# Reordering the opening of a fused attention and feed-forward kernel, and moving two centrings from ScalarE to GpSimd

## The chip, the cores and the metric

The kernel runs on one core of one Trainium2 chip. A core has five engines that each work through their own list of instructions in order and wait for each other through semaphores: TensorE (PE, matrix products; PEld is its weight load), VectorE (DVE), ScalarE (ACT), GpSimd (POOL) and SyncE (SP, which only issues transfers here). The metric is the device time of one launch in microseconds (us); lower is better.

## What is computed

With `x` of 2048 rows by 256, a context of 1601 rows by 192 and 16 heads of 64:

```python
x = x + xattn(layernorm(x), context, mask)   # 16 heads; one learned null key and value in front: 1602 keys
x = x + ffn(layernorm(x))                    # three layers with weights +1/-1: 256 -> 1024 -> 1024 -> 256

# xattn: q = (layer_norm(x) * g_norm) @ Wq ; k, v = split(context @ Wkv)
#        out = softmax(q k^T * 64**-0.5, masked) @ v @ Wout, then layer_norm(out) * g_out
```

Everything is float32 (`fp32r` marks operands rounded for a faster matrix product).

## The kernel before

**Tiling.** The 16 heads are taken as 8 pairs (p), the 2048 rows as 4 blocks (b) of 512: 32 units (p, b), in the order of the list `units`. The 1602 keys are 13 tiles of 128 (KC = 13; the last holds 66). For every unit the kernel needs, ahead of time, an upper bound of each row's scores, so that the exponential does not overflow. These maxima are computed by rounded products in chunks of 512 keys (`max_chunk`, TensorE line 400, then a reduction on VectorE, line 403). Chunk n belongs to query tile n // 3 and key chunk n % 3; `REST` (12) is the last 66 keys of all four tiles.

**One unit of the main loop** (from line 679 on) runs over the 13 key tiles. In step k TensorE writes the scores of a key tile (`scores`, line 442) into one of two buffers `sT`, ScalarE takes the exponential (`exps`, line 468) into one of 13 buffers `e`, TensorE computes one maximum chunk of the *next* unit, and GpSimd adds `e` into the accumulator `acc` for the softmax denominator (lines 720 and 722 inside the loop for tiles 1 to 7, line 728 after it for tile 0 and tiles 8 to 12). The score buffers alternate, so the scores of step k + 2 cannot start before the exponential of step k is done. Tile 0 of the exponentials holds the last, partly filled key tile and is first multiplied on ScalarE by the factor `spent` (line 726). After the loop follow the weighted values (`weighted`, line 475, 52 products), the division by the denominator of the unit before, its output projection, and the projections for coming units.

**What orders the work.** All engines' orders are written out by hand inside `manual_schedule()`; nothing is planned. Two one-element copies to `seen` on ScalarE are there for their waits. The second (line 711) reads one element of the *previous* unit's `acc`, and as ScalarE works in order, everything behind it waits until the last addition into that `acc` is done. It stands before step k = 2 in units 3 to 27 and before step k = 8 in the others (line 710).

**The denominator** of the previous unit is handled in one of two ways (line 746). `quarters` puts it across partitions by `denominators` (line 499), a reciprocal of 256 columns (line 511) and eight copies on ScalarE (line 517). Otherwise `divided` (line 524) makes it with wider products, three key tiles into the weighted values, and one reciprocal of 512 columns (line 526). Before, unit 1 uses `divided`.

**The opening** (lines 629 to 678) prepares unit (0, 0): the keys in three pieces (`first_keys`), the values in two halves (`values_begun`, `values_ended`), the maxima of block 0 in between, and the centring of row block 1 (`second_summed` on ScalarE, `second_normed` on GpSimd). Blocks 2 and 3 are centred in units 0 and 1: VectorE sums them (`input_root`), ScalarE takes the root (a table load, line 535), and `centred_beside` (lines 145 and 146) subtracts and scales with eight ScalarE instructions. `input_turned` (line 556) then transposes the block on TensorE at the end of the same unit. `masked_counted` (lines 428 to 432) counts masked keys by a small product, a VectorE reduction and three GpSimd instructions, and gives `spent`; before, it is the last step of the opening. The maxima use two PSUM buffers (`flex`); keys, values, transposes and scores of the opening share two others (`spare`).

Of the kernel before, what the change touches and what calls it, by code (L numbers as in the profile page):

```python
# [12 lines left out]
AF = mybir.ActivationFunctionType  # L13
# [25 lines left out]
def xattn_ffn(ctx, tc, x, ctxT, mask, g_norm, null_kv, wq, wkv, wout, g_out, k0, k1, k2, s0, s1, s2, out):  # L39
# [108 lines left out]
    with ExitStack() as att:  # L148
# [46 lines left out]
        def project_q(p, b, get=flex, part=None):  # L195

            if part is not None:
                if part == 0:
                    halves["q"] = get(f"psq_{p}_{b}")
                ps = halves["q"]  # L200
                nc.tensor.matmul(
                    ps[:, 0, :], weights[p][0][:, part, :], xnT[:, b, part, :], start=part == 0, stop=part == 1
                )
                if part == 0:
                    return
            qT = wp.tile([128, 512], F32, tag="qT", name=f"qT_{p}_{b}")
            qr = wp.tile([128, 512], F32R, tag="qr", name=f"qr_{p}_{b}", bufs=1)
            if part is None:
                ps = get(f"psq_{p}_{b}")
            for c in range(2) if part is None else ():  # L210
                nc.tensor.matmul(ps[:, 0, :], weights[p][0][:, c, :], xnT[:, b, c, :], start=c == 0, stop=c == 1)  # L211
            nc.scalar.mul(qr, ps[:, 0, :], DH**-0.5)  # L212
            nc.scalar.mul(qT, ps[:, 0, :], DH**-0.5)
            queries[p, b] = (qT, qr)
# [19 lines left out]
        def first_keys(n, get, part=None):  # L234

            kT, _, kr = pairs[0]
            chunks = (CHUNKS[1], CHUNKS[2]) if n == 1 else (CHUNKS[n],)
            if part != 1:
                halves["k"] = get(f"psk_0_{n}")
            ps = halves["k"]  # L240
            for i, (start, w) in enumerate(chunks):
                if part is None or part == i:
                    nc.tensor.matmul(
                        ps[:, i, :w], weights[0][1][:, 0, :], ctx_a[:, ds(start, w)], start=True, stop=False
                    )
            if part == 0:
# [50 lines left out]

        halves = {}

        def values_begun(p, m, tiles, get=flex):  # L300

            if (p, m) not in halves:
                halves[p, m] = get(f"psv_{p}_{m}").rearrange("p i (t d) -> p (i t) d", d=128)
            for t in tiles:
                nc.tensor.matmul(  # L305
                    halves[p, m][:, t - 8 * m, :],
                    ctx_a[:, ts(t, 128)],
                    weights[p][1][:, 1, :],
                    start=t % 4 == 0,
                    stop=False,  # L310
                    skip_group_check=True,
                )

        def values_ended(p, m):

            v, pv = pairs[p][1], halves[p, m]
            tiles = range(8 * m, min(8 * m + 8, KC))
            for t in sorted(tiles, key=lambda t: (t % 4, t)):
                rows = ts((t - 8 * m) // 4, 64)
                nc.tensor.matmul(  # L320
                    pv[:, t - 8 * m, :],
                    ctx_b[rows, ts(t, 128)],
                    weights[p][2][rows, 1, :],
                    start=False,
                    stop=True,
                    skip_group_check=True,
                )
            w = len(tiles)
            nc.scalar.copy(v[:, ds(8 * m, w), :], pv[:, :w, :])
            if p > 0 and m == 0:  # L330
                nc.gpsimd.tensor_copy(v[0:1, 0, :], nullv)

# [5 lines left out]
        def second_summed():  # L338

            sums = sp.tile([128, 2, 4], F32, tag="sums", name="sums_1", bufs=1)  # L340
            r = sp.tile([128, 4], F32, tag="rstd", name="rstd_x1")
            aside = wp.tile([128, D], F32, tag="aside", name="aside", bufs=1)
            for j in range(4):
                nc.scalar.activation(aside, x_sb[:, 4 + j, :], AF.Identity, accum_out=sums[:, 0, j : j + 1])
            nc.gpsimd.tensor_scalar(sums[:, 0, :], sums[:, 0, :], -1.0 / D, None, ALU.mult)
            for j in range(4):
                nc.scalar.activation(
                    aside, x_sb[:, 4 + j, :], AF.Square, bias=sums[:, 0, j : j + 1], accum_out=sums[:, 1, j : j + 1]
                )
            nc.scalar.activation(r, sums[:, 1, :], AF.Sqrt, bias=eps2_sb, scale=(1.0 + EPS) / D)  # L350
            return sums, r
# [289 lines left out]
        first_queries(1)  # L641
        nc.gpsimd.tensor_copy(kept[:, : KC - 1], mcol_u8[:, : KC - 1])
        nc.gpsimd.tensor_copy(kept[:KLAST, KC - 1 : KC], mcol_u8[:KLAST, KC - 1 : KC])
        mv, r = second_summed()
        max_chunk(0, 0, 6)
        first_keys(1, spare, 0)
        max_chunk(0, 0, 9)
        first_keys(1, spare, 1)
        values_begun(0, 0, range(0, 8), spare)
        max_chunk(0, 0, 1)  # L650
        nc.vector.reciprocal(r, r)
        second_normed(mv, r)
        nc.scalar.activation(warm, eps_sb, AF.Exp)
        max_chunk(0, 0, 4)
        values_ended(0, 0)
        max_chunk(0, 0, 7)
        first_keys(3, spare)
        max_chunk(0, 0, 10)
        values_begun(0, 1, range(8, KC), spare)
        max_chunk(0, 0, 2)  # L660
        values_ended(0, 1)
        max_chunk(0, 0, 5)
        keys_stepped(0)
        values_masked(0, 0)
        values_masked(0, 1)
        input_turned(1, spare)
        max_chunk(0, 0, 8)
        max_chunk(0, 0, 11)
        project_q(0, 1, spare)
        max_chunk(0, 0, REST)  # L670
        odd = spare("sT_0_0_1")
        sT = [spare("sT_0_0_0"), odd]
        scores(0, 0, 1, sT[1])
        max_combined(0, 0)
        max_turned(0, 0)
        scores(0, 0, 0, sT[0])
        masked_counted(flex)
        begin.__exit__(None, None, None)
        last = None
        with tc.manual_schedule():  # L680
            for u, (p, b) in enumerate(units):
# [25 lines left out]

                    nc.scalar.copy(seen[:, 0:1], before[:1, 0, 0:1])
                for k in range(KC):
                    if k == (2 if 2 < u < len(units) - 4 else 8) and last is not None:  # L710
                        nc.scalar.copy(seen[:, 1:2], last[3][:1, 0, 0:1])
                    if k == 0 and u > 0:

                        odd = spare(f"sT_{p}_{b}_1")
                        sT = [spare(f"sT_{p}_{b}_0"), odd]
                    es.append(exps(p, b, k, sT))
                    if nxt is not None:
                        max_chunk(*nxt, order[k])
                    if k == 2:
                        nc.gpsimd.tensor_tensor(acc, es[1], es[2], ALU.add)  # L720
                    elif 2 < k < 8:
                        nc.gpsimd.tensor_tensor(acc, acc, es[k], ALU.add)  # L722
                if nxt is not None:
                    max_combined(*nxt)

                nc.scalar.mul(es[0][64:], es[0][64:], spent[64:, 0:1])
                for k in (0, *range(8, KC)):
                    nc.gpsimd.tensor_tensor(acc, acc, es[k], ALU.add)  # L728
                if nxt is None:
                    norm_begin(0, x_sb, "r")  # L730
                    norm_root(0)
                    norm_end(0, y_sb, x_sb, beside=True)
                if u == len(units) - 2:
# [2 lines left out]
                    norm_end(0, y_sb, y_sb, beside=True)  # L736

                    nc.scalar.activation(warm, eps_sb, AF.Exp)
                if u < 2:
                    input_normed(u + 2, *input_root(u + 2), beside=True)  # L740
                    nc.scalar.activation(warm, eps_sb, AF.Exp)
                if u == 0:
                    nc.sync.dma_start(out=ctx_b[64:, 1:512], in_=ctxT[128:CD, 0:511])


                quarters = last is not None and u not in (1, len(units) - 2, len(units) - 1)
                if quarters:
                    den = flex(f"den_{p}_{b}")[:, 0, :256]
                    denominators(last[3], den)
# [204 lines left out]
```

## Time and profile before

| | us |
|---|---|
| median of 3 runs (1269.84 to 1270.65) | 1270.56 |
| the profiled execution, its own time | 1270.18 |
| its span, first to last instruction | 1268.4 |
| TensorE busy | 1257.9 (99%) |
| GpSimd busy | 1008.5 (80%) |
| VectorE busy | 761.7 (60%) |
| ScalarE busy | 717.9 (57%) |

How to read it: times in a timeline count from the span's start. A row of a timeline joins equal instructions that follow each other; its first number is when the first one starts, the second how long the whole row lasts, and behind "x" stands how many there are. A plain float32 product of TensorE shows as two passes, so `x104` at line 475 is 52 products; a rounded one (fp32r) shows as one. In brackets stands the idle time of the engine before the row, and who ended it. A row of waits gives engine and line, then who was waited for, then the total, the number and the longest.

### The profile page before, as it was taken

How to read it: one execution, taken by the hardware profiler on the slowest of the kernel's cores; microseconds unless marked ns; L12 is line 12 of the kernel's file. 1: busy time of each engine (PE TensorE's matmuls, PEld its weight loads, DVE VectorE, ACT ScalarE, POOL GpSimd, SP SyncE). 2: the span in 40 equal slices, each digit the busy share in tenths (PEclk: the TensorE clock that was granted, in tenths of full speed). 3: DMA queues.
4: the chain of work that ended last, by engine and by line, in shares of the span. 5: the costliest groups of instructions: out<-in, count | busy, mean ns of one | idle time of the engine just before them, and what ended most of it. 6: DMA issues, size and time to landing. Idle time of an engine off the chain costs nothing.

```text
span 1268.4 us, 19642 instructions
## 1 busy us (share of the span) xinstructions
PE 1257.9 (99%) x8332; PEld 644.0 (51%) x8332; DVE 761.7 (60%) x812; ACT 717.9 (57%) x982; POOL 1008.5 (80%) x515
## 2 busy tenths in 40 slices
PE   8999999999999999999999999999999999999998
PEld 5344444444444444444444444444444443788887
DVE  6687766656665566556655666656666793635431
ACT  4776666666666656665666566666666676322120
POOL 5898999899889988998899988998898999701100
PEclk9999999999999999999999999999999999999999
DMA  6000000000000000000000000000000010000000
GB/s 171 1 1 5 1 1 13 5 1 1 13 5 1 1 14 5 1 1 13 5 1 2 13 5 1 1 1 6 1 17 1 1 42 1 1 17 1 17 17 17
DMA packets 16984, 13.46 MB, mean 11 GB/s; under 512 B 3152, under 2 KB 16336, under 8 KB 16896
## 3 DMA queue, kind: packets, MB, share of 16 engines
q1 hardware_dynamic: 15904, 11.21, 3.2%
q8 instruction: 65, 1.06, 0.4%
q10 hardware_dynamic: 656, 0.79, 0.2%
q0 software_dynamic: 336, 0.21, 0.1%
q14 instruction: 23, 0.19, 0.0%
HBM read 10.11 MB, written 2.10 MB: 10 GB/s over the span
## 4 chain that ended last, share of the span: by engine, by line
PE 95%; POOL 2%; ACT 1%; DMA 1%; issue 0%; DVE 0%; SPq 0%; DVEq 0%; POOLq 0%; ACTq 0%
PE sT L442 28%; PE av L475 27%; PE ps L836 12%; PE max L400 7%; PE psq L211 4%; PE po L488 4%; PE ps L867 2%; PE psv L305 2%; PE psk L270 1%; PE den L499 1%; PE sT L466 1%; PE psv L320 1%; POOL acc L728 1%; PE psk L275 1%; PE max L384 1%; PE mt L413 1%
## 5 line engine op out<-in xcount | busy, mean ns | idle before, releaser
L403 DVE TENSOR_REDUCE mx<-max 128x2 f32<-128x1024 f32 x384 | 444.4, 1218 | 86.0 <-PE max L400 82.3
L728 POOL TENSOR_TENSOR acc<-acc,e 128x1024 f32<-128x1024 f32 x192 | 473.1, 2464 | 15.1
L468 ACT ACTIVATE e<-sT 128x1024 f32<-128x1024 f32 x416 | 425.8, 1024 | 87.7 <-PE sT L466 44.3
L442 PE MATMUL sT<-qT,kT 64*128 64x512 f32 x1664 | 444.8, 608 | 1.6 <-ACT e L468 1.3
L722 POOL TENSOR_TENSOR acc<-acc,e 128x1024 f32<-128x1024 f32 x160 | 379.3, 2371 | 12.6
L475 PE MATMUL av<-e,v 128*32 128x512 f32 x3328 | 363.6, 592 | 0.1
L400 PE MATMUL max<-kr,qr 64*128 64x512 f32 x768 | 280.6, 718 | 1.2 <-ACT qr L227 1.0
L475 PEld LDWEIGHTS av<-e,v 128*32 128x32 f32 x3328 | 107.4, 110 | 237.9 <-issue 230.1
L442 PEld LDWEIGHTS sT<-qT,kT 64*128 64x128 f32 x1664 | 134.0, 185 | 132.6 <-ACT e L468 121.0
L720 POOL TENSOR_TENSOR acc<-e,e 128x1024 f32<-128x1024 f32 x32 | 75.6, 2363 | 59.6 <-ACT e L468 59.6
L400 PEld LDWEIGHTS max<-kr,qr 64*128 64x128 f32 x768 | 76.7, 187 | 88.6 <-DVE mx L403 65.2
L517 ACT COPY aoT<-r 32x256 f32<-32x256 f32 x224 | 90.2, 403 | 33.4 <-DVE r L511 31.1
L782 ACT COPY avs<-av 128x512 f32<-128x512 f32 x32 | 18.8, 587 | 145.8 <-PE av L475 145.8
L415 DVE TENSOR_TENSOR mT<-mt,pick 128x512 fp32r<-128x512 f32 x32 | 22.1, 690 | 113.4 <-PE mt L413 112.9
L518 DVE TENSOR_TENSOR aoT<-avs,aoT 128x512 f32<-128x512 f32 x28 | 33.3, 1189 | 94.4 <-ACT aoT L517 94.4
L836 PE MATMUL ps<-h0hi,w 128*128 128x512 f32 x256 | 79.6, 392 | 0.0
L836 PE MATMUL ps<-h0lo,w 128*128 128x512 f32 x256 | 78.9, 389 | 0.0
L124 POOL TENSOR_TENSOR y_sb<-y_sb,gout_sb 128x256 f32<-128x256 f32 x12 | 9.3, 777 | 85.6 <-DVE y_sb L91 85.6
L824 ACT ACTIVATE h1hi<-ps 128x1024 fp32r<-128x1024 f32 x16 | 16.4, 1027 | 99.2 <-PE ps L836 99.2
L212 ACT ACTIVATE qr<-psq 128x512 fp32r<-128x512 f32 x31 | 18.5, 598 | 93.5 <-PE psq L211 91.4
L488 PE MATMUL po<-wo,aoT 128*128 128x256 f32 x256 | 60.5, 379 | 0.0
L825 DVE SCALAR_TENSOR_TENSOR h1lo<-ps,h1hi 128x1024 fp32r<-128x1024 f32 x16 | 19.6, 1224 | 67.0 <-ACT h1hi L824 67.0
(171 smaller groups left out, 1207.8 us busy)
## 6 DMA issues: line engine op xcount, KB each, us to landing
out_x<-o SPq DMA_DIRECT2D x7, 256.0 KB, 2.1
x_sb<-in_x SPq DMA_DIRECT2D x3, 512.0 KB, 5.2
wa<-in_wkv SPq DMA_DIRECT2D x8, 128.0 KB, 2.9
wb<-in_wkv SPq DMA_DIRECT2D x16, 64.0 KB, 2.5
wq<-in_wq SPq DMA_DIRECT2D x8, 128.0 KB, 2.2
wo<-in_wout SPq DMA_DIRECT2D x8, 128.0 KB, 2.1
xnT<-in_k SPq DMA_DIRECT2D x1, 1024.0 KB, 5.7
ctx_a<-in_ctxT SPq DMA_DIRECT2D x2, 256.0 KB, 6.2
```

What stands on the lines that cost most here:

```text
L211: nc.tensor.matmul(ps[:, 0, :], weights[p][0][:, c, :], xnT[:, b, c, :], start=c == 0, stop=c == 1)
L400: nc.tensor.matmul(ps[:, j, :w], qr[rows, ts(t, 128)], kr[rows, ds(start, w)], start=True, stop=True)
L403: nc.vector.tensor_reduce(maxima[p, b][:, t, :, c], ps[:, :, :w], AX.X, ALU.max)
L442: nc.tensor.matmul(ps[:n, j, :], kT[rows, ds(128 * KEY_TILES[k], n)], qT[rows, :], start=k < 2, stop=k >= 2, skip_group_check=k >= 2,)
L468: nc.scalar.activation(e, ps, AF.Exp)
L475: nc.tensor.matmul(av[ts(i, 32), 0, :], v[:n, KEY_TILES[k], ts(i, 32)], e[:n, i // 2, :], start=k == 1, stop=k == 0, tile_position=(0, 32 ...
L488: nc.tensor.matmul(pv[:, t, :], aoT[:, ts(t, 128)], weights[p][3], start=True, stop=True)
L517: nc.scalar.copy(aoT[ds(64 * j + 32 * rows, 32), ts(h, 256)], r[ds(64 * j + 32 * h, 32), :])
L720: nc.gpsimd.tensor_tensor(acc, es[1], es[2], ALU.add)
L722: nc.gpsimd.tensor_tensor(acc, acc, es[k], ALU.add)
L728: nc.gpsimd.tensor_tensor(acc, acc, es[k], ALU.add)
L836: nc.tensor.matmul(ps[:, f, :], w(c)[:, ts(2 * g + f, 128)], parts[part][:, c, :], start=i == 0, stop=i == len(steps) - 1,)
```

## The change

It has five parts.

1. *Opening, order on TensorE.* `first_keys(1)` is called in three parts, around maximum chunks 6 and 9: the first 512 keys come ahead of chunk 6. Chunks 1 and 4 follow each other, and the first half of the values is begun with six tiles ahead of them and two behind. Chunk 2 moves ahead of the second half of the values. The query projection of block 1 is cut in two around chunk `REST`.
2. *Opening, other engines.* The reciprocal for block 1 and `second_normed` move behind chunk 7. The table load for the exponential moves from ahead of the first value copy to behind the last one. The five last value tiles are placed in PSUM as three and two (`places`), so that three row pairs finish them, and are copied in two pieces.
3. *`masked_counted`* leaves the opening and comes after the loop over key tiles of unit 0.
4. *Blocks 2 and 3* (the third and fourth) are centred by four GpSimd instructions that stand behind the addition of tile 0; ScalarE keeps the root and the two table loads.
5. *`seen`* is copied at k = 2 in units 1, 2 and 28 too, and unit 1 uses `quarters`.

The transfers and their order on SyncE and GpSimd stay as they are.

```diff
         first_queries(1)
...
+        first_keys(1, spare, 0)
         mv, r = second_summed()
         max_chunk(0, 0, 6)
-        first_keys(1, spare, 0)
+        first_keys(1, spare, 1)
         max_chunk(0, 0, 9)
-        first_keys(1, spare, 1)
-        values_begun(0, 0, range(0, 8), spare)
+        first_keys(1, spare, 2)
+        values_begun(0, 0, range(0, 6), spare)
         max_chunk(0, 0, 1)
+        max_chunk(0, 0, 4)
+        values_begun(0, 0, range(6, 8), spare)
+        values_ended(0, 0)
+        max_chunk(0, 0, 7)
         nc.vector.reciprocal(r, r)
         second_normed(mv, r)
-        nc.scalar.activation(warm, eps_sb, AF.Exp)
-        max_chunk(0, 0, 4)
-        values_ended(0, 0)
-        max_chunk(0, 0, 7)
         first_keys(3, spare)
         max_chunk(0, 0, 10)
+        max_chunk(0, 0, 2)
         values_begun(0, 1, range(8, KC), spare)
-        max_chunk(0, 0, 2)
+        max_chunk(0, 0, 5)
         values_ended(0, 1)
-        max_chunk(0, 0, 5)
+        nc.scalar.activation(warm, eps_sb, AF.Exp)
...
-        project_q(0, 1, spare)
+        project_q(0, 1, spare, 0)
         max_chunk(0, 0, REST)
+        project_q(0, 1, spare, 1)
...
-        masked_counted(flex)
...
-                    if k == (2 if 2 < u < len(units) - 4 else 8) and last is not None:
+                    if k == (2 if u < len(units) - 3 else 8) and last is not None:
                         nc.scalar.copy(seen[:, 1:2], last[3][:1, 0, 0:1])
...
+                if u == 0:
+                    masked_counted(flex)
                 if nxt is not None:
                     max_combined(*nxt)
 
                 nc.scalar.mul(es[0][64:], es[0][64:], spent[64:, 0:1])
+                if u < 2:
+                    mv, r = input_root(u + 2)
+                    nc.vector.reciprocal(r, r)
+                    nc.scalar.activation(warm, eps_sb, AF.Exp)
                 for k in (0, *range(8, KC)):
                     nc.gpsimd.tensor_tensor(acc, acc, es[k], ALU.add)
+                    if k == 0 and u < 2:
+                        for j in range(4):
+                            t = 4 * (u + 2) + j
+                            nc.gpsimd.tensor_scalar(
+                                y_sb[:, t, :], x_sb[:, t, :], mv[:, j, 0:1], r[:, j : j + 1], ALU.subtract, ALU.mult
+                            )
...
-                if u < 2:
-                    input_normed(u + 2, *input_root(u + 2), beside=True)
-                    nc.scalar.activation(warm, eps_sb, AF.Exp)
...
-                quarters = last is not None and u not in (1, len(units) - 2, len(units) - 1)
+                quarters = last is not None and u not in (len(units) - 2, len(units) - 1)
```

More of the change, by code (lines that the diff above doesn't have):

```diff
@@ L237, in first_keys @@
             chunks = (CHUNKS[1], CHUNKS[2]) if n == 1 else (CHUNKS[n],)
-            if part != 1:
+            if not part:
                 halves["k"] = get(f"psk_0_{n}")
@@ L245, in first_keys @@
                     )
-            if part == 0:
+            if part in (0, 1):
                 return
@@ L298, in xattn_ffn @@
         halves = {}
+        places = {t: t if t < 8 else t - 8 if t < 11 else t - 7 for t in range(KC)}
         def values_begun(p, m, tiles, get=flex):
@@ L305, in values_begun @@
                 nc.tensor.matmul(
-                    halves[p, m][:, t - 8 * m, :],
+                    halves[p, m][:, places[t], :],
                     ctx_a[:, ts(t, 128)],
                     weights[p][1][:, 1, :],
-                    start=t % 4 == 0,
+                    start=places[t] % 4 == 0,
                     stop=False,
@@ L317, in values_ended @@
             tiles = range(8 * m, min(8 * m + 8, KC))
-            for t in sorted(tiles, key=lambda t: (t % 4, t)):
-                rows = ts((t - 8 * m) // 4, 64)
+            for t in sorted(tiles, key=lambda t: (places[t] % 4, t)):
+                rows = ts(places[t] // 4, 64)
                 nc.tensor.matmul(
-                    pv[:, t - 8 * m, :],
+                    pv[:, places[t], :],
                     ctx_b[rows, ts(t, 128)],
@@ L327, in values_ended @@
                 )
-            w = len(tiles)
-            nc.scalar.copy(v[:, ds(8 * m, w), :], pv[:, :w, :])
+            for at, w in ((0, 8),) if m == 0 else ((8, 3), (11, 2)):
+                nc.scalar.copy(v[:, ds(at, w), :], pv[:, ds(places[at], w), :])
             if p > 0 and m == 0:
```

## The prediction

> **What bounds the kernel now.** The page comes first: TensorE is busy almost throughout.
>
> ```profile
> PE 1257.9 (99%) x8332; PEld 644.0 (51%) x8332; DVE 761.7 (60%) x812; ACT 717.9 (57%) x982; POOL 1008.5 (80%) x515
> ```
>
> So the change can win no more than TensorE's waits, and its work. The list of TensorE's waits says how much that is:
>
> ```profile
> PE sT L442 <- ACT e L468: 1.3, 5, 0.5
> ...
> PE max L400 <- ACT qr L227: 1.0, 2, 0.6
> PE psq L211 <- ACT xnT L557: 0.6, 1, 0.6
> PE psv L305 <- ACT v L329: 0.3, 1, 0.3
> PE mt L413 <- DVE mcol L408: 0.3, 1, 0.3
> PE max L400 <- DVE mx L403: 0.2, 1, 0.2
> ```
>
> By TensorE's timeline the reordered stretch (14 to 34 us) holds 0.47 (half of the L227 row), 0.20, 0.33 and 0.26: 1.26 together. The 0.53 at 35.8, for the first exponential, stays: its order is unchanged.
>
> Third, GpSimd's timeline in units 0 and 1, then ScalarE's:
>
> ```profile
> 38.09 2.36 POOL L720 TENSOR_TENSOR acc<-e,e 128x1024 f32<-128x1024 f32 x1 [2.73 <-ACT e L468]
> 40.53 12.17 POOL L722 TENSOR_TENSOR acc<-acc,e 128x1024 f32<-128x1024 f32 x5
> 52.77 16.18 POOL L728 TENSOR_TENSOR acc<-acc,e 128x1024 f32<-128x1024 f32 x6
> 70.49 2.36 POOL L720 TENSOR_TENSOR acc<-e,e 128x1024 f32<-128x1024 f32 x1 [1.53 <-ACT e L468]
> ```
>
> ```profile
> 49.45 1.15 ACT L726 ACTIVATE e<-e,spent 64x1024 f32<-64x1024 f32 x1
> ...
> 68.23 7.96 ACT L468 ACTIVATE e<-sT 128x1024 f32<-128x1024 f32 x7 [0.24 <-PE sT L466]
> 76.09 0.17 ACT L711 COPY seen<-acc 1x1 f32<-1x1 f32 x1
> ```
>
> GpSimd's twelve additions of unit 0 run without a gap from 38.09 to 68.95. In unit 1 ScalarE's second exponential (first of the x7) ends at 69.25, and the copy to `seen` stands at 76.09, with 7 us of room. Moved to k = 2, it would stand at 69.25: room 0.3 us.
>
> **Part 1, the opening.** I carry TensorE's changed order forward with the durations of before.
> - The first half of the keys goes behind the query product (13.6), which fills the 0.47. The keys end at 17.7, before 18.26.
> - Six value tiles (of eight in 1.98: 1.50) end at 19.15. Chunk 1 needs rounded keys: VectorE 0.75 from 17.8, GpSimd's cast 0.62: start 19.35. Wait 0.2.
> - Chunks 1 and 4 (0.57), values (1.36), chunk 7 (0.43), last keys (0.73), chunk 10 (0.43): 22.85. Chunk 2 needs the buffer of chunk 7, whose reduction is VectorE's third (3 x 1.14) after chunk 1 is ready at 19.83: 23.4. Wait 0.55.
> - Values (1.31), chunk 5 (0.43), three row pairs (0.45), transposes (0.95), chunks 8 and 11 (0.86): 27.9. The value copy is no longer waited for.
> - But the table load (1.28, from row L653) now stands ahead of the product for `xnT`: copies to 27.0, load and warming to 28.3, `xnT` (0.69) 29.0. Wait 1.15.
> - Query product, chunk REST, scores, without `count` (0.34): the first L466 starts at 33.7, before 34.11.
>
> The gain is **0.4** for the exponentials of unit 0 and for GpSimd behind them. TensorE gets `count` back at the end of the loop, so it stands only 0.1 earlier there. I take 0.45 and 0.15; bounds are a loss of 0.3 and all 1.26.
>
> **Part 2, GpSimd in unit 0.** Three things enter the row of 52.77.
> - `spent` is now made behind the sixth addition. Its rows:
>
> ```profile
> 34.50 0.32 POOL L430 TENSOR_SCALAR spent<-spent,ident 128x1 f32<-128x1 f32 x1 [1.69 <-DVE spent L429]
> 34.90 0.46 POOL L432 TENSOR_TENSOR spent<-spent,ident 128x1 f32<-128x1 f32 x2
> ```
>
>   34.50 to 35.36 is 0.86. VectorE's reduction (0.17) is ready by 50 and hidden.
> - ScalarE's product with `spent`, which ran at 49.45 unseen, now starts only after this, and GpSimd's addition of tile 0 waits for it: 1.15 and two handovers of 0.05, **1.25**.
> - Four centrings. The nearest row has the same shape:
>
> ```profile
> 22.20 2.17 POOL L356 TENSOR_SCALAR y_sb<-x_sb,sums,rstd_x 128x256 f32<-128x256 f32 x4 [1.77 <-issue]
> ```
>
>   **2.15**. Their root follows: product to 54.4, table 1.28, root 0.3, reciprocal 56.2, before the addition of tile 0 ends. VectorE's masking of the context (1.82, L435) waits for that reciprocal and moves too. Before, it held up the addition at 52.77, which took 4.05 instead of 2.43; I keep the 1.6 once, bounds 0 and twice.
>
> Sum: 68.95 - 0.45 + 0.86 + 1.25 + 2.15 = **72.8** for the end of `acc`, moved by 3.8.
>
> The centred block is ready at about 60.7 at the latest, and TensorE's transposes (from 59.7) want the last tile at 60.4: at most 0.5 of waiting, in which case unit 1 starts 0.35 later. Eight ScalarE instructions (L145, L146; 3.9 us) go, beside weighted values of 11.3: worth nothing.
>
> **Part 3, the new wait.** In unit 1 ScalarE comes to `seen` at 69.1 to 69.6 and stands until 72.8. Behind it all further exponentials queue. The third takes 0.13 + 1.02 more: 74.0. TensorE, which has written the scores of step 3, may not begin those of step 4 before that; before, it began them at 70.67 (step 3's chunk ends there). So the third exponential is late last, and TensorE stands **3.35** later. Nothing returns it: TensorE needs 1.16 a step, ScalarE 1.02, so TensorE remains the bound.
>
> In unit 1 `acc` starts at 74.05 and takes 29.6 + 2.15: 105.8. ScalarE's copy of unit 2 is then due at 103.88 + 2.9 = 106.8: no second stall, 1 us of room. The centred block 3 is ready by 94, TensorE wants it at 96.5. Unit 28: `acc` ends at 961.95, second exponential at 962.83, no wait.
>
> **Part 4, quarters in unit 1.** From the chain of waits, the denominator of unit 1 and that of unit 2:
>
> ```profile
> 83.02 1.01 PE den L524 x4
> ...
> 115.79 0.57 PE den L499 x8
> ```
>
> TensorE wins **0.44**. VectorE exchanges 3.34 + 2.15 for 1.75 + 2.86; ScalarE adds eight copies (3.30), done near 94, where the eight centrings were. The result is wanted at 97.8. Hidden.
>
> **Sum.** 3.35 - 0.44 = **2.9 slower**. Against the profiled execution's 1270.18: 1273.1. The median of the runs is 0.4 above that execution, so I say **1273.5**. 0.2% (2.54 us, limits 1268.0 and 1273.1) is about what a measurement of this kernel can tell from no change.
>
> **The clock.** At the end of the run, TensorE idles:
>
> ```profile
> 1264.50:1267.40 2.90, 0.01 (x1) 0.00 (x0) 0.87 (x2) 0.00 (x0) 0.00 (x0) 1.00 0.27 90
> 1267.40:1268.40 1.00, 0.00 (x0) 0.00 (x0) 0.00 (x0) 0.00 (x0) 0.00 (x0) 0.52 0.00 0
> ```
>
> Columns are the stretch, its length, busy time of PE, PEld, DVE, ACT and POOL, and the granted clock. It falls to half after 2.9 us of idleness. TensorE's gap from 5.58 to 6.71 did not lower it. The new gap is some 3 us, so it may. The price is in the opening: passes of `idle` came every 0.21 us from 1.38 to 4.50 and every 0.11 behind, so a return from half speed loses half of 3.1, that is 1.6 us.
>
> [...]
>
> **Rivals.**
> - *The clock halves* behind the stall: 2.9 + 1.6, **1275.1**. For it: 2.9 us sufficed above. Against it: there the gap was not followed by work. Chance 0.28.
> - *The opening gains all its waits*, 1.26: GpSimd's chain ends 0.8 earlier, 2.1 slower, **1272.7**, within 0.2%. Against it: the table load ahead of `xnT`. Chance 0.15.
> - *Other side: the copy to `seen` does not end last.* The change would not stall if the copy needed an earlier addition alone, since one element is read, or if `acc` ended before 69.6, which takes 3.2 us from the 3.8. Then TensorE has -0.15 - 0.44 and up to 0.35: **1270.3**. For it: before, no such copy ever waited visibly. Against it: every addition writes the whole of `acc`, the last too. Chance 0.12.
> - Faster by over 0.2% would take 2.54 where the waits and 0.44 give 1.7: 0.03.
>
> **Chances.** The forecast's own case has 0.42, spread over 1272.5 to 1274.3 by the bounds of the opening and the masking; 0.29 of it lies above 1273.1. Slower: 0.29 + 0.28 = 0.57. Faster 0.03. Same 0.40. The range 1271.6 to 1276.2 takes in the forecast, the clock case with its bounds and most of the second rival: 0.83.
>
> **What would show it.** Right: a wait on ScalarE ahead of the copy to `seen` in unit 1, some 3 us, put down to GpSimd's `acc`; as much on TensorE ahead of the scores of step 4; GpSimd idle for about 1.2 us ahead of the addition of tile 0 in unit 0; TensorE waiting about 1 us for `xnT` near 28; no waits on `seen` in units 2 and 28. Wrong: `acc` of unit 0 ending before the second exponential of unit 1 does, or TensorE idling elsewhere. A granted clock below 1 near 75 us shows the first rival.

## The result and the profile after

| | before | after |
|---|---|---|
| median, us (6 runs each) | 1270.64 (1269.84 to 1272.52) | 1275.92 (1275.47 to 1277.15) |
| the profiled execution, its own time | 1270.18 | 1275.83 |
| its span | 1268.4 | 1274.0 |
| mean granted clock of TensorE | 1.000 | 0.997 |

The ratio is 1.0041, with a 95% interval of 1.0028 to 1.0054: **slower by 0.41%**. That is the forecast's sign and inside its range (1271.6 to 1276.2), but 2.4 us above its number.

The page of the changed kernel: the busy rows, and the clock in 40 slices.

```profile
PE 1259.6 (99%) x8336; PEld 644.6 (51%) x8336; DVE 752.4 (59%) x810; ACT 714.1 (56%) x982; POOL 1017.3 (80%) x523
...
PEclk9989999999999999999999999999999999999999
```

TensorE is busy for 1.7 us longer, though its work hardly changed (four product passes more). The third digit of the clock row says why: between 64 and 96 us it did not run at full speed throughout. The rest of the 5.6 us of span is waiting. TensorE's list of waits in the changed kernel (who waited for whom, total, times, longest):

```profile
PE sT L444 <- ACT e L470: 2.7, 7, 1.2
PE xT L558 <- POOL y_sb L742: 2.3, 3, 0.8
...
PE psq L201 <- ACT xnT L559: 1.3, 1, 1.3
...
PE max L402 <- DVE rstd_x L658: 0.5, 1, 0.5
PE max L402 <- POOL kr L260: 0.4, 1, 0.4
PE psk L243 <- DMA wa<-in_wkv: 0.4, 1, 0.4
```

The wait of 3.35 us that the forecast rests on is not there. In its place stands a row that it did not have: three waits of the transposes (L558) for the block that GpSimd now centres. GpSimd's timeline of the changed kernel, from the new count to the end of `acc` of unit 0:

```profile
53.27 0.32 POOL L432 TENSOR_SCALAR spent<-spent,ident 128x1 f32<-128x1 f32 x1
53.68 0.46 POOL L434 TENSOR_TENSOR spent<-spent,ident 128x1 f32<-128x1 f32 x2
55.39 2.37 POOL L738 TENSOR_TENSOR acc<-acc,e 128x1024 f32<-128x1024 f32 x1 [1.25 <-ACT e L732]
57.75 6.43 POOL L742 TENSOR_SCALAR y_sb<-x_sb,mv_x,rstd_x 128x256 f32<-128x256 f32 x4
64.16 12.07 POOL L738 TENSOR_TENSOR acc<-acc,e 128x1024 f32<-128x1024 f32 x5
```

The count (0.87) and the wait behind it (1.25) are as forecast. The four centrings are not: 6.43 us, and in unit 1, where nothing else lengthens them, 4.83:

```profile
94.48 4.83 POOL L742 TENSOR_SCALAR y_sb<-x_sb,mv_x,rstd_x 128x256 f32<-128x256 f32 x4
```

So `acc` ends at 76.23 instead of 72.8, and the centred tiles come 1.2 us apart. TensorE at that place, in the changed kernel:

```profile
61.83 0.44 PE L558 MATMUL xT<-ident,y_sb 128*128 128x128 f32 x2 [0.76 <-POOL y_sb L742]
...
65.49 3.78 PE L211 MATMUL psq<-xnT,wq 128*128 128x512 f32 x4 [0.35 <-ACT xnT L559]
69.06 2.40 PE L270 MATMUL psk<-ctx_a,wa 128*128 128x401 f32 x4
```

The same two products in the kernel before:

```profile
61.57 1.98 PE L211 MATMUL psq<-xnT,wq 128*128 128x512 f32 x4 [0.56 <-ACT xnT L557]
63.39 1.51 PE L270 MATMUL psk<-ctx_a,wa 128*128 128x401 f32 x4
```

In the changed kernel the query product (L211) starts 3.92 later and takes 3.78 instead of 1.98; the key product (L270) takes 2.40 instead of 1.51. Busy times of the engines by stretch show why (columns: stretch, length, busy of PE, PEld, DVE, ACT and POOL, granted clock, DMA):

```profile
60.60:64.00 3.40, 1.35 (x10) 0.60 (x6) 0.00 (x0) 0.59 (x1) 3.40 (x3) 1.00 0.00 0
64.00:70.90 6.90, 6.32 (x10) 3.03 (x11) 1.35 (x2) 1.83 (x4) 6.74 (x4) 0.51 0.00 0
70.90:76.00 5.10, 5.10 (x30) 2.55 (x30) 3.38 (x4) 2.05 (x2) 4.94 (x3) 1.00 0.00 0
```

Three short waits with transposes between them leave TensorE busy for 1.35 us of 3.40; the clock then halves for 6.83 us. ScalarE in the changed kernel:

```profile
54.17 1.14 ACT L732 ACTIVATE e<-e,spent 64x1024 f32<-64x1024 f32 x1 [4.25 <-POOL spent L434]
...
76.26 0.19 ACT L715 COPY seen<-acc 1x1 f32<-1x1 f32 x1 [0.45 <-POOL acc L738]
...
111.42 0.19 ACT L715 COPY seen<-acc 1x1 f32<-1x1 f32 x1 [1.48 <-POOL acc L738]
```

TensorE has lost so much by then that the copy to `seen` of unit 1 waits for 0.45 only. The same copy in unit 2 (111.42), for which the forecast had 1 us of room, waits for 1.48, since the centring of unit 1 is 2.7 us too long as well.

From before to after, place by place (the later start of the same instruction in the two profiled executions):

| place | later by, us | added there |
|---|---|---|
| unit 0, weighted values | 0.83 | 0.39 a later landing of weights, 0.33 `count`, 0.11 opening |
| unit 1, query product | 3.92 | 3.09 late centred tiles |
| unit 1, first scores | 6.56 | 2.64 half clock |
| unit 1, scores of step 4 | 6.92 | 0.36, at `seen` |
| unit 1, end of weighted values | 6.06 | -0.86 quarters |
| unit 2, weighted values | 7.30 | 1.24, at `seen` |
| unit 7 | 7.33 | 0.24 at `seen` in unit 4, -0.22 |
| units 8 to 31 | 5.60 | -0.22 at the start of most pairs, -0.62 at unit 28 |

### The profile page after: what moved, and what is told of

It is laid out like the page before. It is cut to its first block, busy times and chain, and to the rows that moved or that the text cites. A ratio compares the mean times of both kernels' runs of the same rounds, so it can differ in the third digit from the quotient of the medians.

```text
span 1274.0 us, 19643 instructions
## 1 busy us (share of the span) xinstructions
PE 1259.6 (99%) x8336; PEld 644.6 (51%) x8336; DVE 752.4 (59%) x810; ACT 714.1 (56%) x982; POOL 1017.3 (80%) x523
## 4 chain that ended last, share of the span: by engine, by line
PE 89%; POOL 7%; ACT 1%; DMA 1%; issue 1%; DVE 0%; SPq 0%; DVEq 0%; POOLq 0%; ACTq 0%
PE sT L444 27%; PE av L477 25%; PE ps L849 11%; PE max L402 6%; PE po L490 4%; PE psq L211 4%; POOL acc L738 3%; PE ps L880 2%; POOL acc L726 2%; PE psv L307 2%; PE psk L270 1%; PE den L501 1%; PE sT L468 1%; PE psv L322 1%; ACT e L470 1%; POOL y_sb L742 1%
## 5 line engine op out<-in xcount | busy, mean ns | idle before, releaser
L519 ACT COPY aoT<-r 32x256 f32<-32x256 f32 x232 | 93.4, 403 | 34.0 <-DVE r L513 31.6
L520 DVE TENSOR_TENSOR aoT<-avs,aoT 128x512 f32<-128x512 f32 x29 | 29.8, 1029 | 97.7 <-ACT aoT L519 97.7
L490 PE MATMUL po<-wo,aoT 128*128 128x256 f32 x256 | 60.6, 379 | 0.0
```

The source lines that it names most:

```text
L490: nc.tensor.matmul(pv[:, t, :], aoT[:, ts(t, 128)], weights[p][3], start=True, stop=True)
L519: nc.scalar.copy(aoT[ds(64 * j + 32 * rows, 32), ts(h, 256)], r[ds(64 * j + 32 * h, 32), :])
```

## The experiments

Times are given as distances to the kernel before as it was measured beside each run (medians 1270.28, 1270.27 and 1270.7), with the ratio and its 95% interval. After is 5.28 above its own.

| run | what | us | ratio |
|---|---|---|---|
| a1_add | after, centring in another form | +3.42 | 1.0021 (1.0012 to 1.0030) |
| e1_copied | after, the same form, mean copied | +6.36 | one run |
| c1_filler | after, TensorE kept at work between transposes | +5.86 | 1.0045 (1.0032 to 1.0057) |
| a2_seen8 | after, `seen` late in units 1 and 2 | +3.67 | 1.0026 (1.0016 to 1.0036) |
| a4_count | after, count in the opening | +4.01 | 1.0031 (1.0019 to 1.0042) |
| g1_both | a1 and a2 together | -0.82 | 0.9996 (0.9988 to 1.0005) |
| b1_opening | before, new opening and row pairs | -1.12 | 0.9991 (0.9982 to 0.9999) |
| b2_pairs | before, row pairs alone | -1.80 | 0.9985 (0.9976 to 0.9993) |
| c2_load | b1, table load later | -1.97 | 0.9982 (0.9973 to 0.9991) |
| b3_quarters | before, quarters in unit 1 | +5.86 | 1.0043 (1.0031 to 1.0055) |
| d1_best | the parts that pay | -3.15 | 0.9975 (0.9966 to 0.9984) |
| d3_beside | d1, centring on ScalarE | +2.53 | 1.0020 (1.0012 to 1.0029) |

**The theory** after seeing the profile ("slow form"): GpSimd's subtract-and-multiply is slower than the add-and-multiply whose row gave the forecast its 2.15; it makes the block late, and that starves TensorE and halves its clock. **The rival** ("chain"): the lateness of `acc` and the copy to `seen` set the time of unit 1 whatever the transposes and the clock do.

### a1_add: the centring in the form of the row that priced it

```diff
+                    nm = sp.tile([128, 4], F32, tag="nm", name=f"nm_x{u}")
+                    nc.vector.tensor_scalar(nm, mv[:, :, 0], -1.0, None, ALU.mult)
...
-                                y_sb[:, t, :], x_sb[:, t, :], mv[:, j, 0:1], r[:, j : j + 1], ALU.subtract, ALU.mult
+                                y_sb[:, t, :], x_sb[:, t, :], nm[:, j : j + 1], r[:, j : j + 1], ALU.add, ALU.mult
```

> The changed kernel, with the four GpSimd centrings written as add of the negated mean and multiply (the form of the fast row, 0.54 us each) instead of subtract and multiply; VectorE makes the negated mean with one small instruction. Theory 'slow form': the four take 2.2 us, or 3.8 in unit 0 with the context mask between them, instead of 4.8 and 6.4; the transposes of block 2 no longer wait three times 0.76 us, the clock stays full through them, and the accumulator of unit 0 ends near 73.6 instead of 76.2. Then the wait at the copy to seen in unit 1 that I forecast appears in full: some 3.3 us on TensorE ahead of the scores of step 4, none in unit 2. Time near 1272.5 with a full clock, near 1274 if this gap halves it. Rival 'the form does not matter': the rows stay at 1.2 us each and the time at 1275.9.

Measured: +3.42. GpSimd's row in a1_add, unit 0:

```profile
57.75 3.66 POOL L744 TENSOR_SCALAR y_sb<-x_sb,nm_x,rstd_x 128x256 f32<-128x256 f32 x4
```

3.66 with the masking of the context in it, against 6.43. In unit 1 it is 2.17, against 4.83:

```profile
92.83 2.17 POOL L744 TENSOR_SCALAR y_sb<-x_sb,nm_x,rstd_x 128x256 f32<-128x256 f32 x4
```

The transposes wait no more, and what comes next is the wait of the forecast, in full. TensorE in a1_add:

```profile
74.66 2.08 PE L444 MATMUL sT<-qT,kT 64*128 64x512 f32 x4 [2.99 <-ACT e L470]
```

`acc` ends at 73.47 and `seen` stands at 73.50: the forecast's 72.8 is 0.7 off. Then the clock halves from 73.99 for 6.83 us (scores take 2.08 instead of 1.09). So the slow form caused the late block, and without it the forecast's own wait and its first rival both come.

### e1_copied: the operation, or where its mean lies

```diff
-                                y_sb[:, t, :], x_sb[:, t, :], mv[:, j, 0:1], r[:, j : j + 1], ALU.subtract, ALU.mult
+                                y_sb[:, t, :], x_sb[:, t, :], nm[:, j : j + 1], r[:, j : j + 1], ALU.subtract, ALU.mult
```

(`nm` here is a plain copy of the means.)

> One look at the slow form: the changed kernel with the centrings still subtract and multiply, but with the mean copied into the same small tile that the add form reads. If the operation is slow, the four rows of unit 1 stay at 4.8 us (1.2 each) and the time at 1275.9. If the place of the mean (every second element of the tile of means and variances) was slow, they fall to 2.2 us and the time to 1273.7.

Measured: +6.36, one run. GpSimd in e1_copied, unit 1:

```profile
95.12 4.83 POOL L744 TENSOR_SCALAR y_sb<-x_sb,nm_x,rstd_x 128x256 f32<-128x256 f32 x4
```

The same 4.83 with the same operands as in a1_add's 2.17. It is the pair of operations: 1.20 us for one of 128 x 256 with subtract and multiply, 0.54 with add and multiply.

### c1_filler: does the clock decide?

```diff
+                for _ in range(3 if b == 2 and j > 0 else 0):
+                    nc.tensor.matmul(pts[1][:, 1, ts(j, 128)], ident, ident, start=True, stop=True)
```

> The changed kernel, with three extra products of the identity ahead of each of the last three pairs of transposes of block 2, into places that the transposes overwrite, so that TensorE has work where it waited 0.76 us for GpSimd. Theory 'clock': the 6.8 us at half clock behind these waits cost 2.7 us, and the time falls by as much, to 1273.2. Rival 'chain': the accumulator of unit 0 still ends at 76.2, so what the full clock wins (unit 1 reaches the copy to seen near 73.0 instead of 75.8) is waited for there, and the scores of step 4 start at 77.4 as before; TensorE then idles some 3 us there and the time stays within 0.4 us of 1275.9.

Measured: +5.86. The clock stayed at full speed through the transposes, the first scores of unit 1 came 3.21 later than before instead of 6.56, and nothing was won. TensorE in c1_filler:

```profile
76.86 2.08 PE L444 MATMUL sT<-qT,kT 64*128 64x512 f32 x4 [2.97 <-ACT e L470]
```

TensorE came to `seen` earlier and waited there until `acc` was done; then the clock halved anyway, from 76.25 for 6.83 us. The rival holds for the total: two gates (places where TensorE is held) stand in series, and freeing the first only moves the loss to the second.

### a2_seen8: the second gate removed alone

```diff
-                    if k == (2 if u < len(units) - 3 else 8) and last is not None:
+                    if k == (2 if 2 < u < len(units) - 3 else 8) and last is not None:
```

> The changed kernel, with the copy to seen back at step 8 in units 1 and 2 (unit 28 stays at step 2). Theory 'chain, spread out': the waits of 0.19 us (unit 1) and 1.22 us (unit 2) on TensorE go, but GpSimd stays behind and units 3 and 4, whose copy is at step 2, pay some of it: 1 us faster, 1274.9. Rival: nothing is paid later, 1.4 us faster. Other rival: the exponentials wait for the same additions one by one, no gain.

Measured: +3.67, 1.6 less than after, more than the 1.0 and 1.4 expected. The lateness is not gone: GpSimd is still behind in unit 4, where `seen` is at k = 2 again. TensorE in a2_seen8, unit 4:

```profile
176.27 1.13 PE L444 MATMUL sT<-qT,kT 64*128 64x512 f32 x4 [0.92 <-ACT e L470]
```

In this profile the three waits of 0.77 at the transposes are there too, and the clock stayed full. That is not the usual case: of the eight runs two, this one among them, have a mean granted clock of 1.000 (1273.14 and 1273.15), and six have 0.996 or 0.997 (1273.63 to 1275.4). The section on the hardware comes back to that.

### a4_count: one of the three delays undone

```diff
+        masked_counted(flex)
...
-                if u == 0:
-                    masked_counted(flex)
```

> The changed kernel, with the count of masked keys back at the end of the opening. GpSimd then goes from the sixth addition of unit 0 to that of tile 0 without the 0.86 us for spent and the 1.25 us of waiting for ScalarE's product. Theory 'chain': the accumulator of unit 0 ends 2.1 us earlier, near 74.2, block 2 is centred 2 us earlier, so that the transposes lose 1.6 instead of 3.1 us; unit 1 then waits for the accumulator, and the time is 1274.3, 1.6 below. Theory 'clock': with two gaps of 0.76 us left the clock still halves, and the gain is the 2.1 us of the block alone or less, down to 1273.8; if it stays full, the accumulator takes the gain and the time is as by the chain.

Measured: +4.01, 1.3 less than after; the time, 1274.29, is that of the theory 'chain', though in its trace the clock halves as well (for 3.41 us). The count no longer delays GpSimd; one transpose waits for 0.77 instead of three, and then the wait at `seen` is back. GpSimd's addition of tile 0, and TensorE, in a4_count:

```profile
53.52 3.96 POOL L737 TENSOR_TENSOR acc<-acc,e 128x1024 f32<-128x1024 f32 x1
```

```profile
75.61 1.41 PE L444 MATMUL sT<-qT,kT 64*128 64x512 f32 x4 [3.00 <-ACT e L470]
```

With the count in the opening, VectorE's masking of the context (L437) meets the addition, as it did before (3.96 instead of 2.37); with the count behind the loop it meets the centrings (6.43 instead of 4.83; in after the first of the four takes 2.83, the other three 1.21 each, and the masking runs beside that first one, from 57.06 to 59.44). In both it holds GpSimd up by 1.6, once, as forecast. The traces show the two side by side; why the one holds the other up they do not show.

### g1_both: both gates opened

The edits of a1_add and a2_seen8 together, in after:

```diff
-                    if k == (2 if u < len(units) - 3 else 8) and last is not None:
+                    if k == (2 if 2 < u < len(units) - 3 else 8) and last is not None:
...
-                                y_sb[:, t, :], x_sb[:, t, :], mv[:, j, 0:1], r[:, j : j + 1], ALU.subtract, ALU.mult
+                                y_sb[:, t, :], x_sb[:, t, :], nm[:, j : j + 1], r[:, j : j + 1], ALU.add, ALU.mult
```

> The changed kernel with both repairs: the centrings in the add form and the copy to seen at step 8 in units 1 and 2. Theory 'chain': neither the transposes nor the copy to seen has anything left to wait for, the clock stays full, and what remains is the opening with its late table load (0 to 0.6 us lost) against quarters (0.7), row pairs (1.5) and unit 28 (0.4), with some tenths lost in unit 4: 1268.4, that is 7.5 us below the changed kernel although the two repairs alone gave 2.2 and 2.0. Rival 'they add': 1275.9 - 2.2 - 2.0 = 1271.7.

Measured: -0.82, no different from before by its interval. Alone, the faster form saves 1.9 and the later `seen` 1.6, 3.5 together; both at once save 6.1, where 'chain' said 7.5 and 'they add' 4.2. That is what two gates in series do: each repair alone is partly eaten by the other gate and by the halved clock, which stays in some runs of a1_add and most of a2_seen8 (a mean clock of 0.998 or less in four of eleven and in six of eight; the traces without a halving have 0.999 or 1.000). With both open the clock of its trace stays full from 6.28 us to the end, and unit 1 begins its weighted values 1.09 later than before, against 7.23 in after. A new wait of 0.7 for `aoT` (L490) in unit 1 is part of what is left. One of its twelve runs, of 1274.68, still has a mean clock of 0.996; why stays open.

### b2_pairs, b1_opening, c2_load: the opening, taken apart

b2_pairs is before with `places` and the copies in two pieces alone:

```diff
+        places = {t: t if t < 8 else t - 8 if t < 11 else t - 7 for t in range(KC)}
...
-                    halves[p, m][:, t - 8 * m, :],
+                    halves[p, m][:, places[t], :],
...
-            w = len(tiles)
-            nc.scalar.copy(v[:, ds(8 * m, w), :], pv[:, :w, :])
+            for at, w in ((0, 8),) if m == 0 else ((8, 3), (11, 2)):
+                nc.scalar.copy(v[:, ds(at, w), :], pv[:, ds(places[at], w), :])
```

b1_opening has the new order of the opening as well (count, centring, `seen` and unit 1 as before); c2_load is b1_opening with this:

```diff
         values_ended(0, 1)
-        nc.scalar.activation(warm, eps_sb, AF.Exp)
...
         input_turned(1, spare)
+        nc.scalar.activation(warm, eps_sb, AF.Exp)
         max_chunk(0, 0, 8)
```

> The kernel before with the three row pairs alone, in the opening and the seven later pairs of heads. Theory 'missed gain': 0.22 us less of TensorE for each, 7 or 8 times, less what unit 4 waits for GpSimd, whose accumulator ended there 0.1 us ahead of the copy to seen: 1268.8. Rival: TensorE wins it, but the second copy on ScalarE (0.3 us more) holds back the next exponential, and nothing is left: 1270.3.

> The kernel before with the new order of the opening and the five last values in three row pairs (also in the seven later pairs of heads, since the function is shared); the count of masked keys, the centrings, seen and unit 1 stay as before. Forecast's working: the exponentials of unit 0 start 0.4 us earlier by the opening's order. The changed kernel's trace: the opening gains nothing, since the waits for xnT (1.25), keys (0.42) and chunk 2 (0.47) replace the old ones; unit 0 starts between 0.1 earlier and 0.2 later. Both: the three row pairs, which the forecast counted in the opening alone, save 0.22 us in each of seven later units, 1.3 to 1.5 us in all: time 1268.8 to 1269.0, or 1268.4 with the opening's gain.

> The first of these kernels (new opening, row pairs) with the table load of the exponential moved behind the two products for xnT. If the load's 1.28 us ahead of xnT are what TensorE waits 1.25 us for, that wait goes to below 0.2 us and the time falls by 1.0 to 1.2 us against the kernel without this move, to 1267.8. Rival: the load then stands ahead of the rounding of the queries, which is wanted only after another 3 us, so nothing takes its place; if something does, the time stays at 1268.9.

Measured: -1.80, -1.12 and -1.97. The row pairs work in every pair of heads, not only in the opening. The end of the last five value tiles of a later pair, in before and then in b2_pairs (nine of the ten passes in this row):

```profile
165.78 1.04 PE L320 MATMUL psv<-wb,ctx_b 64*128 64x128 f32 x9
```

```profile
165.46 0.82 PE L322 MATMUL psv<-wb,ctx_b 64*128 64x128 f32 x9
```

0.22 less. b2_pairs is 0.32 earlier in unit 0, and gains some 0.22 at the first unit of most later pairs (0.10 at one, 0.44 at unit 28): 1.97 in its trace. The forecast counted the opening's alone. The new order itself costs 0.7 (b1 against b2), and the table load behind the last value copy is the reason. ScalarE and TensorE in the changed kernel:

```profile
27.56 1.28 ACT L666 ACT_TABLE_LOAD   x1
```

```profile
29.69 1.12 PE L201 MATMUL psq<-xnT,wq 128*128 128x512 f32 x2 [1.25 <-ACT xnT L559]
```

With the load behind ScalarE's products for `xnT` (c2_load) this wait is gone and 0.85 comes back. By the medians the reorder is then worth about 0.2 (c2 against b2), less than the runs can tell. In the trace of c2_load the wait for the keys of chunk 1 is 1.30, because GpSimd's rounding of them stands behind a step that waits for a block of `x`, which landed later in that execution (ScalarE's first row on it starts at 16.83, against 15.62 in d1_best). In the traces of d1_best and d3_beside, which have the same opening and wait 0.3 there, the weighted values of unit 0 start 0.74 and 0.77 earlier than before, 0.4 more than in b2_pairs.

### b3_quarters, d3_beside: what the move to GpSimd is for

b3_quarters is before with `quarters` in unit 1 alone:

```diff
-                quarters = last is not None and u not in (1, len(units) - 2, len(units) - 1)
+                quarters = last is not None and u not in (len(units) - 2, len(units) - 1)
```

> The kernel before with quarters in unit 1 alone, ScalarE still centring there. Forecast's term: TensorE wins 0.44 (1.01 for the wide denominator less 0.57), and the eight copies are hidden. Changed kernel's trace: 0.7, as the wide denominator also interrupts the weighted values. Rival: ScalarE now has eight centring instructions and eight copies (7 us) behind one another, comes late for the copy of the weighted values and for xnT, and TensorE waits for it: up to 1 us slower than by the sum, 1270.3 to 1271.0 instead of 1269.6 to 1269.8.

Measured: +5.86, the largest miss of all. ScalarE, then TensorE, in b3_quarters:

```profile
93.39 3.28 ACT L517 COPY aoT<-r 32x256 f32<-32x256 f32 x8
```

```profile
98.40 3.19 PE L488 MATMUL po<-wo,aoT 128*128 128x256 f32 x8 [3.87 <-DVE aoT L518]
```

ScalarE centres the block until 91.97 and loads the table until 93.3; only then come the eight copies that quarters need, and VectorE after them. TensorE wants the result at 94.5 and waits until 98.4; the clock then halves from 99.04 for 3.41 us. Up to the end of the weighted values quarters win 0.71 (0.51 late becomes 0.20 early).

d3_beside is d1_best (below) with the centring on ScalarE as before:

```diff
-                if u < 2:
-                    mv, r = input_root(u + 2)
-                    nc.vector.reciprocal(r, r)
...
-                    if k == 0 and u < 2:
-                        for j in range(4):
...
+                if u < 2:
+                    input_normed(u + 2, *input_root(u + 2), beside=True)
+                    nc.scalar.activation(warm, eps_sb, AF.Exp)
```

> The fastest kernel so far, with blocks 2 and 3 centred on ScalarE as before instead of on GpSimd in the add form. If the move to GpSimd is worth what it lets ScalarE do in unit 1 (the eight copies for quarters beside the table loads), this is slower by the wait of TensorE for xnT and for the division there, 0.5 to 1 us: 1267.6 to 1268.1. If ScalarE has room for both, the times are the same, 1267.1.

Measured: +2.53, with the same wait of 3.9 for `aoT`; 0.5 to 1 us was the most expected. Against d1_best the move to GpSimd is worth 5.7 us, but only beside `quarters` in unit 1: c2_load, which has neither, is only 1.2 slower than d1_best (which also copies `seen` at k = 2 in unit 28). So the eight ScalarE instructions that I costed at "nothing" are what clears ScalarE for the copies.

### d1_best: the parts that pay

c2_load with the centring on GpSimd in the add form, quarters in unit 1, `seen` at k = 2 in unit 28 too but at 8 in units 1 and 2, and the count left in the opening. Against c2_load:

```diff
-                    if k == (2 if 2 < u < len(units) - 4 else 8) and last is not None:
+                    if k == (2 if 2 < u < len(units) - 3 else 8) and last is not None:
...
+                    if k == 0 and u < 2:
+                        for j in range(4):
+                            t = 4 * (u + 2) + j
+                            nc.gpsimd.tensor_scalar(
+                                y_sb[:, t, :], x_sb[:, t, :], nm[:, j : j + 1], r[:, j : j + 1], ALU.add, ALU.mult
+                            )
...
-                    input_normed(u + 2, *input_root(u + 2), beside=True)
...
-                quarters = last is not None and u not in (1, len(units) - 2, len(units) - 1)
+                quarters = last is not None and u not in (len(units) - 2, len(units) - 1)
```

> The kernel with the moved table load, and besides: blocks 2 and 3 centred on GpSimd in the add form (2.2 us each), quarters in unit 1, the copy to seen at step 2 in unit 28 but at step 8 in units 1 and 2, the count of masked keys in the opening. Theory 'GpSimd's chain matters only through seen': with 7 us of room at step 8 the centrings cost nothing, quarters win 0.7, unit 28 wins 0.4: 1 us below the kernel with the moved load alone, 1266.7, and the clock stays full. Rival 'late accumulator comes due': GpSimd starts unit 1 some 1.5 us late and pays in unit 3 or 4, where the kernel before had 0.1 us of room, up to 1 us: 1267.7.

Measured: 1267.12 (1266.67 to 1269.16), -3.15 against before, so about 8.4 below after. It beats both, and lies between the theory's 1266.7 and the rival's 1267.7; the rival's late accumulator does not show in its trace, where units 3 and 4 lose nothing. TensorE is busy for 1255.9, against 1257.9 before. `acc` of unit 0 ends at 70.24, the clock stays at full speed to the end of the work, and once the opening's products have begun no wait in TensorE's list is longer than 0.6.

## Why the prediction was right, and where it was wrong

**Right.** The sign, and the mechanism it named: the additions into `acc` of unit 0 end later than ScalarE's early `seen` of unit 1 can bear. `spent` (0.86 forecast, 0.87), the wait behind it (1.25, 1.25), the masking's 1.6 once, and in the opening the waits for `xnT` (1.15, 1.25), for the keys of chunk 1 (0.2, 0.42) and at chunk 2 (0.55, 0.47; the forecast named VectorE's third reduction, where the profile names the reciprocal that stands there). With the centring at its forecast price (a1_add), `acc` ends at 73.47 and TensorE waits 2.99 at step 4, where 72.8 and 3.35 were forecast. In the changed kernel itself that wait is not what sets the time: by the table it is worth 0.36 in unit 1, and the prediction's own sign of being wrong, "TensorE idling elsewhere", came true at the transposes.

**The step that failed** is Part 2's third item: "Four centrings. The nearest row has the same shape", priced at 2.15. The row L356 has the shape but adds and multiplies; L742 subtracts and multiplies, and takes 4.83. What hangs on it was then sized wrongly:
- "At most 0.5 of waiting" at the transposes became 2.3, and 3.09 with what follows.
- The halved clock, the first rival, came true, but at the transposes instead of behind `seen`, and at 2.64 instead of 1.6, for it lasted two stretches of 3.41 us. With the centring repaired it comes where it was put, behind `seen` (a1_add). That the sum kept the clock full behind a gap of some 3 us, and gave the halving a chance of 0.28, was an estimate, and no trace shows such a gap without a halving: 2.99 in a1_add, 2.97 in c1_filler and 3.00 in a4_count each came with one.
- The wait of 3.35 at `seen` fell to 0.36, because TensorE had lost 5.7 since unit 0 already; c1_filler shows it coming back to 2.97 as soon as the transposes cost less clock. Unit 2, for which it said "no second stall", stalled for 1.22.

**The opening** was to bring the first exponential 0.4 forward. After has it 0.11 later, its weights' later landing set aside; in the four traces with the same opening and no such landing (c1_filler, e1_copied, g1_both, a2_seen8) it lies between 0.10 earlier and 0.09 later. So nothing was gained. The three waits were seen, and came to 2.14 in after where the sum had 1.9. Part of the rest is the query projection cut in two: its halves take 1.05 each from row to row, where the whole took 1.91 before.

**Missed on the other side.** Row pairs in the seven later pairs, 1.65 us in the trace of b2_pairs; k = 2 in unit 28, where 0.62 was won and b1_opening, with k = 8 there, won 0.44; and 0.71 instead of 0.44 for quarters (b3_quarters). These 2 us, which the forecast did not reckon with, are why the time is still within the range, so that is in part luck: the losses of units 0 to 4 (the positive rows of the table, 0.83 + 3.09 + 2.64 + 0.36 + 1.24 + 0.24) come to 8.4, where the forecast had 3.35, and without the 2 us the time would, by this reckoning, lie near 1278, above 1276.2.

**The parts were not independent.** The sum gave Part 2's removed ScalarE work nothing and Part 4 a free place. b3_quarters shows the free place was made by Part 2: quarters without it cost 5.9, where the forecast's reasoning, and mine ahead of the run, gave a small gain or loss.

The 0.39 us by which the first weights landed later belongs to the execution and not to the change: the wait for them stands in the traces of after, a1_add, b1_opening and b3_quarters (which has the opening of before), and in no other. Not tried: the new order of the opening with all else of after unchanged and the table load moved; b1_opening and c2_load answer for it on the kernel before.

## What to carry to other kernels

Price a moved operation by a row with the same operation, not only the same shape and engine; if none exists, let the range run to the slowest row of that engine. Where two waits stand in series, a repair of one shows only a part until the other is repaired too, so test them together before calling either harmless. And before costing removed work at nothing, ask which instruction added elsewhere in the same change needs its place.

## What the runs showed of the hardware

**GpSimd's price here depended on the pair of operations**: 1.20 us for subtract and multiply on 128 x 256 float32, 0.54 for add and multiply, with the same operands (e1_copied, a1_add).

**The clock halved without a wholly idle stretch.** The changes of TensorE's granted clock lie on a grid of 3.41 us: in before it is full for 1262.93 us, 370 times 3.413; in after full for 58.03, half for 6.83 and full for 1201.49, which is 17, 2 and 352 times; and the halvings of the table last 3.41 or 6.83. I laid this grid, from each trace's own changes, over TensorE's recorded work, counting as idle what no recorded product covers:

| run | stretch from | idle of 3.41 | clock of the next | idle in that one | half for |
|---|---|---|---|---|---|
| after | 60.60 | 2.07 | half | 0.57 | 6.83 |
| a1_add | 70.58 | 2.32 | half | 0.67 | 6.83 |
| c1_filler | 72.84 | 2.37 | half | 0.60 | 6.83 |
| a4_count | 72.92 | 2.69 | half | 0.00 | 3.41 |
| b3_quarters | 95.62 | 2.78 | half | 0.00 | 3.41 |
| d3_beside | 94.22 | 2.91 | half | 0.00 | 3.41 |
| a2_seen8 | 59.13 and 62.54 | 1.42 and 1.44 | full | | |
| e1_copied | 59.21 and 62.62 | 1.53 and 1.32 | full | | |
| e1_copied, later | 72.86 | 2.28 | half | 0.70 | 6.83 |

Read this way, a stretch with 2.07 idle was enough, and so was one with 1.90 at the end of g1_both's trace; one with 1.53 was not (where the bound lies between them stays open); and the clock came back after one stretch when that was busy throughout, after two when 0.57 or more of the first was idle. So the same three waits of 0.77 at the transposes halve the clock in after and not in a2_seen8 and e1_copied, where the grid cuts them in two. The grid's place differs from trace to trace (the first change of the clock comes at 4.50 us in before, 5.99 in after and 6.28 in g1_both), and in a1_add the times go with the clock: its eleven runs lie between 1271.3 and 1275.02, the two lowest at a mean granted clock of 1.000, the three highest at 0.997. That it is the grid's place that parts these runs is likely but not shown, since only one of them has a trace; and not all spread comes from it, for the slowest run of a4_count (1275.27) has a mean of 1.000.
